# Second layer norm's refinements on VectorE, W's norm asked for sooner, and two instead of three ph products ahead of the first group of batch 0

## The chip, the cores and the metric

The kernel runs on one core of a Trainium2 chip. The metric is the device time of one execution in microseconds; the median of three runs of the kernel before is 919.04 us (917.95 to 919.18). Of the core's engines, TensorE does the matrix products, VectorE and ScalarE the elementwise work, GpSimd some very small elementwise work, and SyncE (SP) does no arithmetic: its queue issues every DMA of this kernel.

## The reference

A layer norm, a product with a context through a fake quantisation to 8 bits, a residual, a second layer norm, and a feed-forward product with bias, to which a routed low-rank part (the best two of eight experts) is added, with a second residual:

```python
q1 = fake_quant(layernorm(x), x1_scale, x1_zp)
q2 = fake_quant(ctx, x2_scale, x2_zp)
x = x + matmul(q1, q2)
xf = layernorm(x)
w = top2(softmax(xf @ W_router.T))
h = einsum('td,erd->ter', xf, lora_A)
lora_out = einsum('ter,eor,te->to', h, lora_B, w) * 2.0
x = x + xf @ W_base.T + b_base + lora_out
```

There are two batches of 1024 rows; all widths are 2048, in float32.

## The kernel before

The two batches run one after the other. A batch's 1024 rows are eight tiles of 128 rows, and two neighbouring tiles make a pair p (0 to 3). The columns are in two halves of 1024.

**First product.** In batch 0, `gemm1` (L772) takes tile after tile; `evac1` adds the result to x. In batch 1, `gemm1w` (L886) does it pairwise with fewer products. When the last columns of a tile are in, the sums for the second layer norm are there.

**Second layer norm.** `ln2` (L911) works on a pair p. Its `stat` (L920 to L927) makes mean and variance with a few VectorE instructions on a column or two, and a first guess of the reciprocal root (`seed`, L451). Its `newton` (L933) refines the guess in three steps (`rstd_steps`, L462) and then makes the scale `a` and the offset `mb` (L937 to L939). The line `fast = p >= 2` puts this on VectorE for pairs 2 and 3, one tile at a time, and on GpSimd for pairs 0 and 1, both tiles at once. A refinement step takes four instructions on GpSimd, three on VectorE for two tiles, and two on VectorE for one.

**y and its transposes.** `y_prep` (L943) makes seven matrices of each pair from its four quarters of y = (x - mean) * scale: a11 and a12 from the first tile, then a22, and the combinations s1 to s4 by VectorE (`comb`, L973). Each is split into a hi and a lo part in float16 (the lo part by VectorE, L965), named nat_... , and both are transposed by DMA into y_... (L407 for a half, L969 for a whole).

**Weights.** A piece of W is named by batch, half of W, group and k: w_0_0_2_6 belongs to batch 0, half 0, group 2, k = 6. `w_step` (L1136) loads its parts (wn, wt, wb, wc), combines them, and splits the scaled result: hi at L417 or L424, lo at L1158 on VectorE. The scale gW comes from the norm of W's half: `w_norm` (L601) loads sixteen pieces wn_15 to wn_0, sums their squares, adds them up over the partitions with a TensorE product wsum, and computes gW, uW and sB. It is called with a time: `w_norm(0, t - WN0)`, where t is the planned end of the first product.

**Feed-forward product.** `g2` (L1339) goes through two halves f, four groups in each, eight k in a group and four pairs; each is three matmuls of 128x512 into a PSUM bank X or Y. In the first half, group 0 takes a11 and a12 of y, group 1 s2 and s1, group 2 s3 and s4, group 3 a22. The bias is loaded as bb and added at L1267 in group 2.

**The ph products.** `hmm` (L1004) makes the router's and low-rank part's product ph_b_i of tile i (L1014, L1018; 32 matmuls, in two halves). For an even tile it takes a11 and a12, for an odd tile s1 and a22. `HFIRST[b]` names the tiles whose product stands ahead of the first group, `HLATE[b]` those which follow at the start of group 1 of the first half.

**What sets the order.** No engine's list is written by hand. Every piece of work is a task with an engine, an estimated duration and the buffers it reads and writes (`Plan.add`, L123). `rank` gives each a due time from those who need it, back from times given for TensorE's work, and `order` (L177) then lays out all five engines' lists by these due times while the kernel is built. Each engine executes its list strictly in order. So an estimate, a due time or the engine of one task can move others on every engine. SP's queue is such a list too: loads, stores and transposes wait for each other's turn, and each DMA uses one of eight lanes in rotation.

Of the kernel before, what the change touches and what calls it, by code (L numbers as in the profile page):

```python
# [18 lines left out]
ALU = mybir.AluOpType  # L19
# [6 lines left out]
D = 2048  # L26
# [16 lines left out]
         "sm": 4, "sm2": NP, "wacc": 1, "ps": 8}  # L43
HORIZON = 120.0
MM = 0.216
SPREAD = .75
LANES = 8
DEPTH = 2.5
NEAR = 45.0
WARM = 90  # L50
WFAR = 90.0
HFIRST = ((0, 1, 2), (0, 2, 4))
HLATE = ((4, 6, 3, 5, 7), (6, 1, 3, 5, 7))
EV1 = 5.0
QBOTH = 2
EV1W = 2.0
# [18 lines left out]
WKEEP0 = 8  # L75
PUT_W = 10
WN_STEP = 3.0
WN0 = 20.0
WN1 = 40.0
SPILL0 = 3  # L80
SP_T = 5.0
# [36 lines left out]
class Plan:  # L118
# [4 lines left out]
    def add(self, eng, dur, fn, r=(), w=(), prio=None, cap=None, dma=None, far=None, turn=False,  # L123
            store=False):
        t = Task()
        t.durs = eng if isinstance(eng, dict) else {eng: dur}
        t.eng, t.dur = None, min(t.durs.values())
        t.fn, t.prio, t.cap, t.dma = fn, prio, cap, dma
        t.preds, t.succs, t.bufs = set(), [], []
        t.seq, t.ready, t.start, t.done = len(self.tasks), 0.0, None, None  # L130
        if self.lead is not None:
            t.cap = self.lead
        t.pe = prio if eng == "PE" else None
        t.far, t.turn, t.store = far, turn, store
        t.whole = t.mate = None
        t.skip = False

        def spans(accs):
            for a in accs:
                buf, parts = a if isinstance(a, tuple) else (a, None)  # L140
                if buf not in t.bufs:
                    t.bufs.append(buf)
                    buf.users += 1
                for i in range(buf.parts) if parts is None else parts:
                    yield buf, i

        for buf, i in spans(r):
            last, readers = buf.state[i]
            if last is not None:
                t.preds.add(last)  # L150
            readers.append(t)
        for buf, i in spans(w):
            last, readers = buf.state[i]
            if last is not None:
                t.preds.add(last)
            t.preds.update(readers)
            buf.state[i] = (t, [])
        t.preds.discard(t)
        for p in t.preds:
            p.succs.append(t)  # L160
        self.tasks.append(t)
        return t
# [165 lines left out]
def xattn_ffn_kernel(ctx, tc, x, cx, scal, wT, bias, arT, bT, out):  # L328
    nc = tc.nc
# [5 lines left out]
    add = plan.add  # L335
# [325 lines left out]
    def ln1(S, b, i):  # L661
# [30 lines left out]
        if b:  # L692
# [8 lines left out]
            for h in range(2):  # L701
# [4 lines left out]
                        "p (k t s) -> p k s t", t=P, s=2),  # L706
                    HD, [(q, [2 + h])], [(aT, [h])], bias=nz1, dve=SPREAD)
        else:
# [18 lines left out]
        if first:  # L727
# [8 lines left out]

            add("PE", 2.0 + MM * WARM / 2, warm_up, w=[warm], prio=0.0)

# [33 lines left out]
    def gemm1(S, b, i, c, t):  # L772
# [3 lines left out]
        def mm(k0, n):  # L776
            for k in range(k0, k0 + n):
                nc.tensor.matmul(  # L778
                    ps.ap(), aT.ap()[:, k, :], S["b", c, k // 4].ap()[:, k % 4, :],
                    start=k == 0, stop=k == KT - 1,  # L780
                )

        n = 2 if b == 0 and c < 1 and i < 4 else 4
        for k0 in range(0, KT, n):
            bp = S["b", c, k0 // 4]
            parts = [k0 % 4 // 2] if n == 2 else [0, 1]
            at = t + k0 * MM
            if n == 2 and c == 0:
                at = t - i * KT * MM + LEAD * i + PACE * k0
            add("PE", n * MM, lambda k0=k0: mm(k0, n), r=[(aT, [k0 // HK]), (bp, parts)], w=[ps],  # L790
                prio=at)
        evac1(S, b, i, c, ps, t + KT * MM + EV1)
        if c % 2:
            squares(S, b, i, c)

    def evac1(S, b, i, c, ps, cap, total=True):
        xb = S["x", i][c // 2]
        p, j = i // 2, i % 2
        if ("s2", p) not in S:
            S["s2", p] = buf("sm2", [P, 52], F32, f"sm2_{b}_{p}", 2)  # L800
        s = S["s2", p]

        def evac():
            xs = xb.ap()[:, (c % 2) * C : (c % 2 + 1) * C]
            o = 14 + 4 * j + c
            kw = dict(accum_out=s.ap()[:, o : o + 1]) if total else {}
            nc.vector.scalar_tensor_tensor(xs, ps.ap(), s12, xs, ALU.mult, ALU.add, **kw)  # L807

        add("DVE", 0.75, evac, r=[ps], w=[(xb, [c % 2])] + ([(s, [j])] if total else []), cap=cap)
# [76 lines left out]
    def gemm1w(S, b, p, cp, grp, t):  # L886
        ops = GROUPS1[grp]
        for j, (bk, op, fresh) in enumerate(ops):
# [4 lines left out]
            for h in range(2):  # L893
# [9 lines left out]

                add("PE", 4 * MM, mm, r=[acc, w], w=[ps], prio=t + (8 * j + 4 * h) * MM)
            for bk2, tt, c, total in EVAC1[grp]:
# [4 lines left out]

    def ln2(S, b, p, js):  # L911
        s = S["s2", p]
        fast = p >= 2
        j0, n = js[0], len(js)

        def cut(o, w=1):
            v = s.ap()[:, o + j0 * w : o + (j0 + n) * w]
            return v if w == 1 else v.rearrange("p (j c) -> p j c", j=n)

        def stat():  # L920
            m, d, v, r, hv = cut(28), cut(30), cut(0), cut(4), cut(6)
            nc.vector.tensor_reduce(m, cut(14, 4), AX.X, ALU.add)
            nc.vector.tensor_reduce(v, cut(24, 2), AX.X, ALU.add)
            nc.vector.tensor_scalar(m, m, 1.0 / D, None, ALU.mult)
            nc.vector.tensor_tensor(d, m, cut(22), ALU.add)
            nc.vector.tensor_tensor(d, d, d, ALU.mult)
            nc.vector.scalar_tensor_tensor(v, v, 1.0 / D, d, ALU.mult, ALU.subtract)  # L927
            seed(v, r, hv)

        add("DVE", 1.5, stat, w=[(s, js)])  # L930

        def newton():
            e = nc.vector if fast else nc.gpsimd  # L933
            r, hv, t = cut(4), cut(6), cut(8)
            rstd_steps(e, r, hv, t, n)
            m, a, mb = cut(28), cut(10), cut(12)
            e.tensor_scalar(a, r, YS, None, ALU.mult)  # L937
            e.tensor_tensor(mb, m, a, ALU.mult)
            e.tensor_scalar(mb, mb, -1.0, None, ALU.mult)  # L939

        add("DVE" if fast else "POOL", 2.0 if fast else 4.8, newton, w=[(s, js)])

    def y_prep(S, b, p):  # L943
        s = S["s2", p]
# [470 lines left out]
    for b in range(NB):  # L1415
        S = {}
        for o in ("x0", "c0", "x1", "x2", "x3", "c1", "x4", "x5", "x6", "x7", "c2", "c3"):
            n = int(o[1])
            if o[0] == "x":
                plan.lead = lead(b, "x", n)  # L1420
                load_x(S, b, n)
                ln1(S, b, n)
                plan.lead = None
            else:
                load_b(S, b, n)
        if b == 0:
            for i, c in unit_order():
                gemm1(S, b, i, c, t)
                t += KT * MM
                if c == NC - 1:  # L1430
                    S["t_y", i] = t
        else:
            for p in range(NP):
                half_sums(S, b, p)
            for cp in range(2):
                half_diffs(S, b, cp)
            for p, cp, grp in BLOCKS1:
                gemm1w(S, b, p, cp, grp, t)
                t += 8 * MM * len(GROUPS1[grp])
                if cp and grp > 1:  # L1440
                    S["t_y", 2 * p + grp - 2] = t
        if b == 0:
            prep_lora(t - LORA_T)
            prep_bmax(t - LORA_T + 20.0)
            w_norm(0, t - WN0)
        for p in range(NP):
            for js in ([0], [1]) if p >= 2 else ([0, 1],):
                ln2(S, b, p, js)
            y_prep(S, b, p)
        for i in HFIRST[b]:  # L1450
            hmm(S, b, i, t)
            t += 2.8
        for f in range(2):
            cp = f if b == 0 else 1 - f
            for i in range(NT):
                reload(S, b, f, cp, i)
            for grp in range(4):
                if grp == 1:
                    if not f:
                        for i in HLATE[b]:  # L1460
                            hmm(S, b, i, t)
                            t += 2.8
                        router(S, b)
                if grp == 2 - f:
                    load_lb(S, b, cp, (1, 0, 2))
                if grp == 2:
                    add_bias(S, b, cp, t + BIAS)
                elif grp == 3:
                    if b == 0 and f == 0:
                        w_norm(1, t - WN1)  # L1470
                for k in range(HK):
                    w_step(S, b, f, cp, grp, k, t)
                    for p in range(NP):
                        lag = LAG3 if p == 3 else 0
                        g2(S, b, f, cp, grp, k, p, t + (0 if f or grp else lag * 24 * MM))
                        t += 3 * MM * len(GROUPS[f][grp])
                        if k == HK - 1:
                            t += 3 * MM * len(LORA[f][grp])
# [55 lines left out]
```

## Time and profile before

| | |
|---|---|
| median of three runs | 919.04 us |
| profiled execution | 917.52 us |
| its span | 915.7 us |
| mean granted TensorE clock | 0.994 |
| GpSimd | busy 67.1 us (7%), 256 instructions |
| ScalarE | busy 399.9 us (44%) |
| TensorE | busy 897.4 us (98%) |
| first matmul of the first group of batch 0 | 150.43 us |

All times in the text that are not durations count from the start of the span. The profile names engines PE (TensorE), PEld (its weight loads), DVE (VectorE), ACT (ScalarE), POOL (GpSimd) and SPq (SP's DMA queue). A row of the timeline has the start, the duration, the engine, the source line, the operation, what it writes and reads, and, in brackets, how long the engine had been idle before it and what ended that. A group row has the busy time and mean duration in ns of one, then the idle time just before such instructions and its commonest cause. Names of buffers stand there without their numbers.

### The profile page before, as it was taken

The page shows a single profiled execution, that of the slowest core. Times are in us where ns is not written, and L with a number is a line of the kernel's source. Part 1 is how long each engine was busy: PE and PEld are TensorE (multiplying, and loading weights), DVE is VectorE, ACT ScalarE, POOL GpSimd, SP SyncE. Part 2 cuts the span into 40 slices and gives each one's busy share as a digit, 9 for nine tenths or more (in the row PEclk, how much of TensorE's full clock was granted, in tenths as well). Part 3 has the DMA queues.
Part 4 walks back from the last instruction along what each step waited for, and adds up shares of the span by engine and source line. Part 5 has one row for each costly group of instructions (what it writes and reads, how often), then busy time and mean ns, then how long its engine had stood idle before and what let it go on. Part 6 is the DMA issues. An engine that isn't in the chain of part 4 may idle for free.

```text
span 915.7 us, 12485 instructions
## 1 busy us (share of the span) xinstructions
PE 897.4 (98%) x4514; PEld 431.3 (47%) x4514; DVE 712.6 (78%) x1271; ACT 399.9 (44%) x454; POOL 67.1 (7%) x256
## 2 busy tenths in 40 slices
PE   7999998999999999999999999899999999999998
PEld 5444445474444444444444444547444444444443
DVE  7999989999599975899899987899734453899131
ACT  5998677516044321414696667853100121234000
POOL 0024220000000000002470001000000000000000
PEclk9999999999999999999999999999999999999999
DMA  8999999997999999999999647999996169793021
GB/s 322 387 386 295 304 275 237 220 227 253 231 332 332 409 375 368 363 376 365 346 350 299 204 164 200 242 201 179 309 234 210 58 208 393 257 347 124 4 91 47
DMA packets 223981, 241.02 MB, mean 263 GB/s; under 512 B 146096, under 2 KB 158384, under 8 KB 223920
## 3 DMA queue, kind: packets, MB, share of 16 engines
q1 hardware_dynamic: 223920, 240.23, 86.6%
q8 instruction: 35, 0.57, 0.3%
q14 instruction: 26, 0.21, 0.1%
HBM read 163.65 MB, written 41.94 MB: 225 GB/s over the span
## 4 chain that ended last, share of the span: by engine, by line
PE 86%; DVE 7%; DMA 4%; issue 1%; POOL 1%; SPq 0%; ACT 0%; DVEq 0%
PE X L1348 36%; PE Y L1348 27%; PE g L778 6%; PE gX L898 5%; PE gY L898 4%; PE ph L1014 2%; PE X L1364 2%; PE Y L1364 2%; DMA bs<-in_cx_dram 1%; PE ph L1018 1%; DMA wn<-in_wT_dram 1%; DVE x L807 1%; DMA y_a<-nat_a 1%; DVE nat_a L965 1%; DMA wc<-in_wT_dram 1%
## 5 line engine op out<-in xcount | busy, mean ns | idle before, releaser
L1348 PEld LDWEIGHTS <-y_s 128*128 128x128 f16 x1536 | 150.2, 98 | 180.8
L1348 PE MATMUL Y<-w,y_s 128*128 128x512 f16 x768 | 206.8, 379 | 0.0
L1348 PE MATMUL X<-w,y_s 128*128 128x512 f16 x768 | 206.5, 379 | 0.0
L1348 PE MATMUL X<-w,y_a 128*128 128x512 f16 x768 | 189.9, 380 | 1.2 <-DVE w L1158 0.7
L1348 PEld LDWEIGHTS <-y_a 128*128 128x128 f16 x1152 | 112.5, 98 | 134.3 <-issue 3.1
L778 PE MATMUL g<-b,at 128*128 128x512 f16 x512 | 114.3, 383 | 4.5 <-ACT b L417 2.5
L417 ACT ACTIVATE w<-wb,gW 128x1024 f16<-128x1024 f32 (+1 forms) x47 | 50.7, 1084 | 128.9 <-DVE wb L1219 56.9
L1348 PE MATMUL Y<-w,y_a 128*128 128x512 f16 x384 | 103.6, 380 | 0.0
L1376 DVE SCALAR_TENSOR_TENSOR xr<-X,uW,xr 128x512 f32<-128x512 f32 x64 | 46.7, 744 | 50.2 <-PE X L1348 25.5
L778 PEld LDWEIGHTS <-at 128*128 128x128 f16 x512 | 49.9, 99 | 64.7 <-issue 4.5
L1158 DVE SCALAR_TENSOR_TENSOR w<-wb,gW,w 128x1024 f16<-128x1024 f32 (+1 forms) x48 | 56.9, 1190 | 7.3 <-ACT w L417 7.2
L1376 DVE SCALAR_TENSOR_TENSOR xr<-Y,uW,xr 128x512 f32<-128x512 f32 x42 | 31.0, 743 | 35.1 <-PE Y L1364 35.0
L417 ACT ACTIVATE b<-u,nz 128x1024 f16<-128x1024 uint8 x40 | 45.0, 1139 | 15.5 <-DVE bt L869 13.8
L467 POOL TENSOR_TENSOR sm<-sm 128x1 f32<-128x1 f32 (+1 forms) x48 | 12.8, 266 | 480.7 <-DVE sm L453 476.9
L417 ACT ACTIVATE w<-wt,gW 128x1024 f16<-128x1024 f32 x14 | 16.1, 1148 | 63.6 <-DVE wt L1205 37.2
L417 ACT ACTIVATE yt_a<-x,sm 128x1024 f32<-128x1024 f32 x28 | 33.4, 1231 | 23.4 <-POOL sm L939 13.7
L440 DVE BATCH_NORM_STATS2 sm<-x 128x6 f32<-128x512 f32 x64 | 40.8, 680 | 3.0 <-DMA x<-in_x_dram 2.9
L417 ACT ACTIVATE nat_s<-yt_a 128x1024 f16<-128x1024 f32 x29 | 30.0, 1050 | 24.8 <-DVE yt_a L973 20.6
L417 ACT ACTIVATE q<-x,sm 128x1024 uint8<-128x1024 f32 x30 | 35.7, 1230 | 11.3 <-POOL sm L677 8.0
L826 ACT ACTIVATE sq<-x,sm 128x1024 uint8<-128x1024 f32 x32 | 36.3, 1136 | 9.0 <-DVE x L807 9.0
L417 ACT ACTIVATE u<-bs,sc,rec 128x1024 uint8<-128x1024 f32 x31 | 38.0, 1231 | 3.6 <-DMA bs<-in_cx_dram 3.4
L1018 PE MATMUL ph<-ar,y_a 128*128 128x136 f16 x192 | 35.3, 225 | 4.2 <-DMA y_a<-nat_a 4.1
(191 smaller groups left out, 1160.9 us busy)
## 6 DMA issues: line engine op xcount, KB each, us to landing
bs<-in_cx_dram SPq DMA_DIRECT2D x64, 512.0 KB, 9.4
wt<-in_wT_dram SPq DMA_DIRECT2D x64, 512.0 KB, 7.2
wn<-in_wT_dram SPq DMA_DIRECT2D x32, 512.0 KB, 9.5
x<-in_x_dram SPq DMA_DIRECT2D x30, 512.0 KB, 8.3
spill<-x SPq DMA_DIRECT2D x28, 512.0 KB, 3.6
xr<-spill SPq DMA_DIRECT2D x28, 512.0 KB, 8.1
wb<-in_wT_dram SPq DMA_DIRECT2D x24, 512.0 KB, 8.0
out_dram<-xr SPq DMA_DIRECT2D x24, 512.0 KB, 5.7
```

What stands on the lines that cost most here:

```text
L417: nc.scalar.activation(o, i, AF.Copy if c is None else AF.Identity, scale=1.0 if a is None else a, bias=0.0 if c is None else c,)
L440: nc.vector.bn_stats(st[:, 2 * h + c], b.ap()[:, c * C : (c + 1) * C])
L467: e.tensor_tensor(t, r, r, ALU.mult)
L778: nc.tensor.matmul(ps.ap(), aT.ap()[:, k, :], S["b", c, k // 4].ap()[:, k % 4, :], start=k == 0, stop=k == KT - 1,)
L826: nc.scalar.activation(sq.ap(), xb.ap(), AF.Square, bias=a[:, 22 + j : 23 + j], accum_out=a[:, 24 + 2 * j + h : 25 + 2 * j + h],)
L898: nc.tensor.matmul(ps.ap(), a()[:, 4 * h + k, :], w.ap()[:, k, :], start=fresh and h + k == 0, stop=h == 1 and k == 3, skip_group_check=True,)
L1014: nc.tensor.matmul(ph.ap()[:, : 2 * AR], y[half].ap()[:, 0, k, :], ar[:, kr, :], start=kk == 0, stop=False,)
L1018: nc.tensor.matmul(ph.ap()[:, AR : 2 * AR], y[half].ap()[:, 1, k, :], ar[:, kr, :AR], start=False, stop=kk == KT - 1,)
L1158: lambda: nc.vector.scalar_tensor_tensor(w.ap()[:, 1, lo:up], src(), g, w.ap()[:, 0, lo:up], ALU.mult, ALU.subtract),
L1348: nc.tensor.matmul(ps.ap(), y.ap()[:, a, k, :], w.ap()[:, q, j * C : (j + 1) * C], start=k == 0 and fresh and i == 0, stop=k == HK - 1 and ...
L1364: nc.tensor.matmul(ps.ap(), hT.ap()[:, 2 * p + tt, a], lb.ap()[:, q], start=fresh and i == 0, stop=i == 2, skip_group_check=True,)
L1376: nc.vector.scalar_tensor_tensor(xs, ps.ap(), uW[:, cp : cp + 1], xs, ALU.mult, ALU.add)
```

## The change

It touches constants at the top, `ln2`, and the loop that calls it.

- The refinement of pairs 0 and 1 goes to VectorE in both batches, still for both tiles at once (`NEWTON`, `SPLIT`).
- The division of the mean by D is folded into the instruction after it, in `stat`, and into the offset in `newton`, where two instructions become one on VectorE. The planner's estimates for the two tasks are lowered by 0.2 each.
- `WN0` is 30 instead of 20: the work of W's first norm is due ten us sooner.
- In batch 0, tile 1's ph product moves from `HFIRST` to `HLATE`, behind tiles 4 and 6.

```diff
--- before.py
+++ after.py
@@ -43,14 +43,16 @@
          "sm": 4, "sm2": NP, "wacc": 1, "ps": 8}
 HORIZON = 120.0
 MM = 0.216
+NEWTON = (0, 0)
+SPLIT = (2, 2)
 SPREAD = .75
 LANES = 8
 DEPTH = 2.5
 NEAR = 45.0
 WARM = 90
 WFAR = 90.0
-HFIRST = ((0, 1, 2), (0, 2, 4))
-HLATE = ((4, 6, 3, 5, 7), (6, 1, 3, 5, 7))
+HFIRST = ((0, 2), (0, 2, 4))
+HLATE = ((4, 6, 1, 3, 5, 7), (6, 1, 3, 5, 7))
 EV1 = 5.0
 QBOTH = 2
 EV1W = 2.0
@@ -75,7 +77,7 @@
 WKEEP0 = 8
 PUT_W = 10
 WN_STEP = 3.0
-WN0 = 20.0
+WN0 = 30
 WN1 = 40.0
 SPILL0 = 3
 SP_T = 5.0
@@ -910,7 +912,7 @@
 
     def ln2(S, b, p, js):
         s = S["s2", p]
-        fast = p >= 2
+        fast = p >= NEWTON[b]
         j0, n = js[0], len(js)
 
         def cut(o, w=1):
@@ -921,13 +923,12 @@
             m, d, v, r, hv = cut(28), cut(30), cut(0), cut(4), cut(6)
             nc.vector.tensor_reduce(m, cut(14, 4), AX.X, ALU.add)
             nc.vector.tensor_reduce(v, cut(24, 2), AX.X, ALU.add)
-            nc.vector.tensor_scalar(m, m, 1.0 / D, None, ALU.mult)
-            nc.vector.tensor_tensor(d, m, cut(22), ALU.add)
+            nc.vector.scalar_tensor_tensor(d, m, 1.0 / D, cut(22), ALU.mult, ALU.add)
             nc.vector.tensor_tensor(d, d, d, ALU.mult)
             nc.vector.scalar_tensor_tensor(v, v, 1.0 / D, d, ALU.mult, ALU.subtract)
             seed(v, r, hv)
 
-        add("DVE", 1.5, stat, w=[(s, js)])
+        add("DVE", 1.3, stat, w=[(s, js)])
 
         def newton():
             e = nc.vector if fast else nc.gpsimd
@@ -935,10 +936,13 @@
             rstd_steps(e, r, hv, t, n)
             m, a, mb = cut(28), cut(10), cut(12)
             e.tensor_scalar(a, r, YS, None, ALU.mult)
-            e.tensor_tensor(mb, m, a, ALU.mult)
-            e.tensor_scalar(mb, mb, -1.0, None, ALU.mult)
-
-        add("DVE" if fast else "POOL", 2.0 if fast else 4.8, newton, w=[(s, js)])
+            if fast:
+                e.scalar_tensor_tensor(mb, m, -1.0 / D, a, ALU.mult, ALU.mult)
+            else:
+                e.tensor_tensor(mb, m, a, ALU.mult)
+                e.tensor_scalar(mb, mb, -1.0 / D, None, ALU.mult)
+
+        add("DVE" if fast else "POOL", 1.8 if fast else 4.8, newton, w=[(s, js)])
 
     def y_prep(S, b, p):
         s = S["s2", p]
@@ -1444,7 +1448,7 @@
             prep_bmax(t - LORA_T + 20.0)
             w_norm(0, t - WN0)
         for p in range(NP):
-            for js in ([0], [1]) if p >= 2 else ([0, 1],):
+            for js in ([0], [1]) if p >= SPLIT[b] else ([0, 1],):
                 ln2(S, b, p, js)
             y_prep(S, b, p)
         for i in HFIRST[b]:
```

## The prediction

> **What bounds the kernel now.** I read the page's busy shares first, then every hole in TensorE's timeline, then, for each hole, the engine or queue that closed it.
>
> ```profile
> PE 897.4 (98%) x4514; PEld 431.3 (47%) x4514; DVE 712.6 (78%) x1271; ACT 399.9 (44%) x454; POOL 67.1 (7%) x256
> ...
> L417 ACT ACTIVATE yt_a<-x,sm 128x1024 f32<-128x1024 f32 x28 | 33.4, 1231 | 23.4 <-POOL sm L939 13.7
> ...
> L1018 PE MATMUL ph<-ar,y_a 128*128 128x136 f16 x192 | 35.3, 225 | 4.2 <-DMA y_a<-nat_a 4.1
> ```
>
> TensorE is idle for 915.7 - 897.4 = 18.3 us. The change can reach neither the first load (6.6) nor the tail after the last matmul (3.8). The rest is three places. The second row says that ScalarE's first y tiles wait for GpSimd's refinement, the third that the ph products wait for transposes of y_a. The timeline of TensorE shows where:
>
> ```profile
> 143.94 0.29 PE L1014 MATMUL ph<-ar,y_a 128*128 128x272 f16 x1 [0.25 <-DMA y_a<-nat_a]
> ...
> 147.53 0.29 PE L1014 MATMUL ph<-ar,y_a 128*128 128x272 f16 x1 [2.02 <-DMA y_a<-nat_a]
> 148.55 0.23 PE L1018 MATMUL ph<-ar,y_a 128*128 128x136 f16 x1 [0.73 <-DMA y_a<-nat_a]
> ...
> 581.18 0.23 PE L1018 MATMUL ph<-ar,y_a 128*128 128x136 f16 x1 [3.36 <-DMA y_a<-nat_a]
> ```
>
> So 3.0 us stand in batch 0 inside ph_0_2, ahead of the first FFN group (150.43), and 3.36 us in batch 1 inside ph_1_2. Two more waits for split weights, 0.51 and 0.67, come at 311. The busy time by stretch, from the view of windows (busy and count of PE, weight loads, DVE, ACT, POOL, then the clock):
>
> ```profile
> 149.20:152.70 3.50, 3.50 (x16) 1.85 (x14) 3.16 (x5) 2.46 (x4) 0.00 (x0) 0.51 1.04 198
> ...
> 260.00:285.00 25.00, 25.00 (x118) 11.33 (x116) 24.55 (x62) 15.12 (x25) 0.00 (x0) 1.00 1.02 334
> ...
> 581.20:584.60 3.40, 3.40 (x35) 2.78 (x36) 0.10 (x1) 1.18 (x2) 0.00 (x0) 1.00 1.13 220
> ```
>
> The first hole is followed by 3.5 us at a clock of 0.51, worth 1.7 us; the hole of batch 1 is not (1.00). And from 260 to 285 VectorE is busy 24.55 of 25 us: TensorE does not wait there, but only just. I took each weight piece's first matmul against the end of its VectorE part: group 1 of batch 0 has 9.5 to 20 us in hand, w_0_0_2_2 (first used at 258.76) 1.22, w_0_0_2_3 0.53, w_0_0_2_6 only 0.04. What starts that stretch is SP's queue and then VectorE:
>
> ```profile
> 222.16 2.00 SPq L969 DMA_TRANSPOSE y_s<-nat_s  x1
> 224.25 0.86 SPq L398 DMA_DIRECT2D xr<-spill  x1
> 225.21 3.58 SPq L407 DMA_TRANSPOSE y_s<-nat_s  x2
> ...
> 246.25 0.54 SPq L398 DMA_DIRECT2D bb<-in_bias_dram  x1
> 246.84 0.45 SPq L398 DMA_DIRECT2D wc<-in_wT_dram  x1
> ```
>
> ```profile
> 251.11 2.36 DVE L1267 TENSOR_TENSOR xr<-xr,bb 128x1024 f32<-128x1024 f32 x2 [1.68 <-DMA bb<-in_bias_dram]
> ```
>
> From 222.16 transposes stand back to back until the bias (bb) and wc_0_0_2_2 are issued, and VectorE idles 1.68 us for the bias. Later here is later for the batch.
>
> **The change part by part.**
>
> *Refinements to VectorE.* The four refinements that move took GpSimd, in its timeline, 6.3 us (93.86 to 100.13) and 7.1 (115.06 to 122.19) in batch 0, 4.2 each (546.43, 560.00) in batch 1. VectorE's refinement of pair 3 runs nine small instructions from 142.16 to 144.03, 0.21 each; for two tiles it is 3 x 3 + 2 = 11, 2.3 us. Four add 9.2; the folded scale removes 12 + 8 instructions, 4.0. So VectorE gains 5.2 us of work, and each pair's scale comes 4.0 to 4.8 us sooner in batch 0 and 1.9 in batch 1, if VectorE is free. Here a rule speaks against the change: the Trainium skill (Perfetto Trace Analysis, Optimizing Scalar/DVE Operations) says that with a saturated VectorE some work may be better off on ScalarE or even GpSimd. Over the stretches where batch 0's refinements land (95 to 136) VectorE is busy 36.9 of 41 us, so by the rule up to 5.2 us could be lost; by the rows TensorE waits for nothing there, the added work fits the 4.1 idle, and its cost is 0. I go by the rows; the rule returns below, at 260 to 285.
>
> *W's norm sooner.* The ten last wn loads of W's half are issued from 110.84 to 119.41, and the two transposes behind them take 12.53 us on SP where the next two take 3.09. Built, the changed order has them ahead of every y transpose; the last would land near 122 instead of 132. The scale gW then hangs on the last layer-norm piece instead: TensorE's first product ends near 139.5, behind it on VectorE come an eviction (0.74), a residual (1.2), statistics (1.2), the scale (1.3), an eviction (0.74), two hi parts (0.75 each) and w_0_0_0_0's lo part (1.28). That gives 146 against 149.45. Bounds 145 and 148.3; I take 146, 3.5 sooner.
>
> *ph_0_1 later.* Its 32 matmuls (140.11 to 142.9, 2.8 us) move to group 1's start; nothing is saved. TensorE would be through ph_0_2 at 150.43 - 3.0 - 0.6 (half clock) - 2.8 = 144, and wait for w_0_0_0_0 until 146. The stall of y_a12_0_1 goes, since its transpose is now ahead by some 12 us; the weight is late next, by 2. Group 0 starts 4.5 sooner, group 1, behind ph_0_1, 1.7 sooner. The clock may keep its full rate too; this cannot show in the end, as the next step says.
>
> *What is pushed behind.* In the changed lists pair 0's y_s1 and y_a22 are made after the first group starts. SP gets their four transposes (1.3 to 2 us each) between 157 and 200, ahead of group 1's weights, whose 9.5 to 20 us cover them. VectorE, between w_0_0_0_0 and w_0_0_1_7 (223.29), gets four combinations and two lo parts of pair 0 (6 x 1.14), pair 3's first refinement (1.9), three pieces of its y (2.1), two ph sums (0.5), one hi part (0.75), less one copy and two moved operations (3.0): 9. It starts 3.5 sooner and has idle time of 2.04 (182.06), 0.27, 0.63 and 0.80 to take it up; since TensorE's end of group 0 comes sooner too, I count 2.7 of 3.7. So w_0_0_1_7 comes at +2.8. Behind it stand, in the changed order, nat_s4_0_0 and a combination of pair 3 (2.3), for which the xr load ahead of y_s4_0_0 waits. y_s4_0_0 is issued at 223.3 + 2.8 + 2.3 + 0.9 = 229.3 instead of 225.21: **+4.1**. Bounds: +0.8 if VectorE takes up everything (then the queue waits for TensorE's end with w_0_0_1_3, 227.68 - 1.7), +6 if it takes up nothing more than 1. From there to w_0_0_2_7 both kernels have the same SP and VectorE lists. w_0_0_2_2 is then ready at 261.7, TensorE arrives at 258.76 - 1.7 = 257.1 and stalls 4.6; at w_0_0_2_6 it is 4.1 late, with no slack left to hide it.
>
> *The clock behind that stall.* The Trainium skill (TensorE: Matmul & The Clock Gate, Why this matters for your kernels) warns of idle gaps over about 3 us, which send the clock to half. Here 3.36 us did not (1.00 after 581.2) and 3.0 in three pieces did. By the rule the 4.6 costs 1.7 more, by the row of batch 1 nothing; since the next weights are late on VectorE anyway, at most about 0.5 of it shows. I take 0.4.
>
> *Batch 1.* y_a12_1_1's last transpose is issued at 577.65, behind lo parts that VectorE did at 570.86 and 571.99 and a spill that waited until 574.49. In the changed order those lo parts stand right behind three evictions and pair 1's refinement, some 4 us sooner, the spill stands behind the transposes, and TensorE has its leftover products between the two halves of ph_1_2. The 3.36 should go: -3.0, bounds -1 (VectorE, 3.53 of 3.7 busy at the hole, too late) and -3.4. The weights of batch 1 have 4 us and more in hand.
>
> Sum: 4.1 + 0.4 - 3.0 = +1.5. The profiled execution took 917.52 (span 915.7, 1.8 around it), 1.5 under the median of 919.04, so it would become 919.0, and the median **920.5**.
>
> **Rivals.**
> - *The queue keeps its time* (other side). VectorE's idle places take up all nine us and y_s4_0_0 slips 0.8 only, so TensorE's slip at w_0_0_2_6 is 0.8 and batch 1 gives 3.4: 919.04 - 2.6 = 916.4. It decides when y_s4_0_0 slips less than 2.6. For it: group 1's weights leave VectorE room; against: it is busy 66.6 of 71.5 us from 150.5 to 222.
> - *Batch 1 keeps its hole, or gets another*, as VectorE is 95% busy ahead of it: +4.5, 923.5. Against: its lists there put the needed lo parts first.
> - *The change only moves the holes*: 2 us of waiting for w_0_0_0_0 and 1 at w_0_0_2_2 for 3.0 and 3.36 with half a gain in batch 1: 919. The slack of 0.04 speaks against a small slip there.
>
> **How the numbers follow.** Forecast 0.50, queue keeps its time 0.28, batch 1 keeps its hole 0.14, moved holes 0.08. What a measurement can tell from no change is about 0.2%, 1.8 us. The forecast's own range is 918.8 to 922.6, with half of it or more beyond the 1.8. With the rivals: 915.8 to 923.6; faster 0.28, same 0.28, slower 0.44.
>
> **What would show it.** Right: no wait for y_a in ph_0_2, a wait of about 2 for w at the first group, a wait of 3 to 5 for w near 257 (L1348, by VectorE L1158), the bias issued near 250, no hole in ph_1_2, GpSimd without 128x2 refinements of the second layer norm. Wrong: bias issued at or before 248, or the hole of batch 1 still there, or a new one for y of pair 3 near 163, where the cover is some 3 us before and less after.

## The result, and the profile after

| | before | after |
|---|---|---|
| median of 6 runs, same chip | 919.11 us (917.95 to 920.15) | 922.69 us (921.18 to 923.51) |
| ratio, 95% interval | 1 | 1.0038 [1.0021, 1.0054] |
| profiled execution, span | 917.52, 915.7 | 921.18, 919.3 |
| granted clock, mean | 0.994 | 0.990 |

The changed kernel is slower by 3.5 us (0.0038 x 919; by the interval 1.9 to 5.0). The page of after, in the rows that answer to those of before (the first is busy us, share and instructions by engine; the other is a group: out<-in, shape, count, then busy us, mean ns, idle us before it and what ended it):

```profile
PE 900.2 (98%) x4514; PEld 432.2 (47%) x4514; DVE 718.0 (78%) x1297; ACT 398.1 (43%) x452; POOL 49.9 (5%) x196
...
L1018 PE MATMUL ph<-ar,y_a 128*128 128x272 f16 x192 | 37.0, 285 | 2.7 <-DMA y_a<-nat_a 2.7
```

VectorE has 5.4 us more (5.2 counted), GpSimd 17.2 less. TensorE's matmuls are the same 4514; they are busy 2.8 us longer, which goes with the lower clock, and its idle time is 919.3 - 900.2 = 19.1 against 18.3. So the holes have moved, not gone. TensorE's timeline of after (start, us, instruction, in brackets the idle time before it and its releaser) has these, and none at the first group:

```profile
255.44 0.38 PE L1352 MATMUL X<-w,y_s 128*128 128x512 f16 x1 [1.83 <-ACT w L419]
257.73 1.01 PE L1352 MATMUL X<-w,y_s 128*128 128x512 f16 x2 [1.92 <-DVE w L1162]
...
586.76 0.29 PE L1018 MATMUL ph<-ar,y_a 128*128 128x272 f16 x1 [2.65 <-DMA y_a<-nat_a]
587.63 0.30 PE L1022 MATMUL ph<-ar,y_a 128*128 128x136 f16 x1 [0.59 <-DMA y_a<-nat_a]
```

The first two are one stall of 3.75 us at w_0_0_2_2, the last two a hole of 3.24 inside ph_1_4, where before had one of 3.36 inside ph_1_2. (In these rows ACT w L419 is ScalarE's hi part of the weight, DVE w L1162 VectorE's lo part.) Read at TensorE's first product of each stage, the difference grows in two places only. (The third column is a second profiled execution of the same changed kernel, taken later.)

| TensorE starts (us) | before | after | after, again |
|---|---|---|---|
| w_0_0_0_0 (first FFN group) | 150.43 | 143.40 | 143.55 |
| w_0_0_1_0 (group 1) | 206.31 | 201.64 | 201.79 |
| w_0_0_2_2 (behind the stall) | 258.76 | 255.44 | 258.01 |
| w_0_0_3_0 | 295.02 | 296.44 | 297.73 |
| w_0_1_0_0 (end of batch 0's first half) | 322.56 | 323.98 | 325.27 |
| w_1_1_1_0 (batch 1) | 641.78 | 645.20 | 647.80 |
| end of the last matmul | 911.95 | 915.37 | 917.97 |

In batch 0 a lead of 7.0 us at the first group, 4.7 at group 1, becomes a loss of 1.4 (again: 2.7). From w_0_1_0_0 to w_1_1_1_0 it takes 319.22 before, 321.22 after (again: 322.53), a loss of 2.0 (3.3). From there to the last matmul all three take 270.17. The third column also shows how far two profiles of one kernel can lie apart: 2.6 us. So below a place is read from profiles, a cost from the ratios.

How the lead is lost shows on SP's queue in after (the same three issues that were shown of before, up to the bias):

```profile
222.22 1.94 SPq L973 DMA_TRANSPOSE y_s<-nat_s  x1
224.49 0.71 SPq L400 DMA_DIRECT2D xr<-spill  x1
225.30 3.73 SPq L409 DMA_TRANSPOSE y_s<-nat_s  x2
...
246.29 0.57 SPq L400 DMA_DIRECT2D bb<-in_bias_dram  x1
```

and in VectorE's timeline, which waits for it:

```profile
251.24 2.36 DVE L1271 TENSOR_TENSOR xr<-xr,bb 128x1024 f32<-128x1024 f32 x2 [6.75 <-DMA bb<-in_bias_dram]
```

The bias is issued at 246.29 where it was 246.25 before: the queue has kept its time to 0.04 us although TensorE is 4.7 ahead, so VectorE idles 6.75 us for it instead of 1.68, and TensorE arrives early at a weight that is not earlier. In the second profile of after it is issued at 248.73.

What sets the queue is the stretch between the first group and those transposes, as far as the traces tell. The view of windows of before, and then of after (length; busy us and count of PE, weight loads, DVE, ACT, POOL; clock; DMA share; GB/s):

```profile
146.00:222.00 76.00, 73.74 (x438) 40.18 (x439) 71.13 (x103) 40.97 (x46) 0.00 (x0) 0.98 1.03 241
```

```profile
146.00:222.00 76.00, 76.00 (x468) 41.93 (x467) 73.79 (x104) 38.66 (x42) 0.00 (x0) 1.00 0.90 217
```

VectorE is busy 73.79 of 76 us (97%), though over the whole span its share is 78%. TensorE does not wait in this stretch either (76.00 of 76). But what SP's queue waits for comes from VectorE, and with VectorE full, TensorE's lead does not make it come sooner. No run changes VectorE's load in this stretch alone, so this reading rests on d1 and a3 below, which move work into and out of it.

The loss from w_0_1_0_0 to w_1_1_1_0 is another matter. The windows of before, and then of after, over just this stretch:

```profile
322.56:641.78 319.22, 315.73 (x1615) 152.70 (x1613) 278.76 (x477) 167.52 (x178) 38.65 (x150) 1.00 0.95 287
```

```profile
323.98:645.20 321.22, 317.44 (x1615) 153.56 (x1614) 283.06 (x492) 166.85 (x177) 32.54 (x120) 0.99 0.95 288
```

Of the 2.0 us only 0.3 is waiting (321.22 - 317.44 = 3.78 against 3.49). The other 1.7 is TensorE being busy longer with the same 1615 products: behind its hole after has 3.41 us at half clock (0.50 from 587.08 to 590.49), and before has none there. More on this under the clock below.

### The profile page after: what moved, and what is told of

It reads as the page before. It is cut to its first block, busy times and chain, and to the rows that moved or that the text cites. A ratio compares the mean times of both kernels' runs of the same rounds, so it can differ in the third digit from the quotient of the medians.

```text
span 919.3 us, 12454 instructions
## 1 busy us (share of the span) xinstructions
PE 900.2 (98%) x4514; PEld 432.2 (47%) x4514; DVE 718.0 (78%) x1297; ACT 398.1 (43%) x452; POOL 49.9 (5%) x196
## 4 chain that ended last, share of the span: by engine, by line
PE 73%; DVE 12%; DMA 6%; ACT 3%; issue 2%; POOL 1%; SPq 1%; DVEq 0%; ACTq 0%; POOLq 0%
PE X L1352 32%; PE Y L1352 24%; PE g L780 7%; PE ph L1018 2%; PE X L1368 2%; PE Y L1368 2%; DVE x L809 2%; PE gX L900 2%; DVE w L1162 1%; DMA wc<-in_wT_dram 1%; PE ph L1022 1%; DMA wt<-in_wT_dram 1%; PE gY L900 1%; DMA bs<-in_cx_dram 1%; DVE sm L442 1%
## 5 line engine op out<-in xcount | busy, mean ns | idle before, releaser
L419 ACT ACTIVATE w<-wb,gW 128x1024 f16<-128x1024 f32 (+1 forms) x46 | 49.6, 1082 | 121.5 <-DVE wb L1223 57.8
L780 PEld LDWEIGHTS <-at 128*128 128x128 f16 x512 | 49.8, 98 | 64.7 <-issue 3.7
L1162 DVE SCALAR_TENSOR_TENSOR w<-wb,gW,w 128x1024 f16<-128x1024 f32 (+1 forms) x48 | 56.8, 1190 | 7.3 <-ACT w L419 7.2
L419 ACT ACTIVATE b<-u,nz 128x1024 f16<-128x1024 uint8 x40 | 45.0, 1139 | 15.3 <-DVE bt L871 13.8
L419 ACT ACTIVATE nat_s<-yt_a 128x1024 f16<-128x1024 f32 x32 | 33.0, 1051 | 30.3 <-DVE yt_a L977 24.0
L419 ACT ACTIVATE w<-wt,gW 128x1024 f16<-128x1024 f32 x14 | 16.1, 1148 | 64.9 <-DVE wt L1209 40.6
L419 ACT ACTIVATE q<-x,sm 128x1024 uint8<-128x1024 f32 x30 | 35.7, 1231 | 11.3 <-POOL sm L679 7.3
L419 ACT ACTIVATE u<-bs,sc,rec 128x1024 uint8<-128x1024 f32 x31 | 38.0, 1232 | 4.7 <-DMA bs<-in_cx_dram 4.1
L1018 PE MATMUL ph<-ar,y_a 128*128 128x272 f16 x192 | 37.0, 285 | 2.7 <-DMA y_a<-nat_a 2.7
L900 PEld LDWEIGHTS <-at 128*128 128x128 f16 x256 | 24.9, 98 | 30.5 <-issue 1.5
L1271 DVE TENSOR_TENSOR xr<-xr,bb 128x1024 f32<-128x1024 f32 x28 | 33.4, 1216 | 6.8 <-DMA bb<-in_bias_dram 6.8
L977 DVE TENSOR_TENSOR yt_a<-yt_a,yt_a 128x1024 f32<-128x1024 f32 x32 | 38.5, 1215 | 0.0
```

The source lines that it names most:

```text
L419: nc.scalar.activation(o, i, AF.Copy if c is None else AF.Identity, scale=1.0 if a is None else a, bias=0.0 if c is None else c,)
L780: nc.tensor.matmul(ps.ap(), aT.ap()[:, k, :], S["b", c, k // 4].ap()[:, k % 4, :], start=k == 0, stop=k == KT - 1,)
L900: nc.tensor.matmul(ps.ap(), a()[:, 4 * h + k, :], w.ap()[:, k, :], start=fresh and h + k == 0, stop=h == 1 and k == 3, skip_group_check=True,)
L977: add("DVE", 1.22, lambda: nc.vector.tensor_tensor(dst.ap(), a.ap(), c.ap(), op), r=[a, c], w=[dst])
L1018: nc.tensor.matmul(ph.ap()[:, : 2 * AR], y[half].ap()[:, 0, k, :], ar[:, kr, :], start=kk == 0, stop=False,)
L1162: lambda: nc.vector.scalar_tensor_tensor(w.ap()[:, 1, lo:up], src(), g, w.ap()[:, 0, lo:up], ALU.mult, ALU.subtract),
```

## The experiments

Each theory's expectation was written before its run. Times are differences from before, from the ratio of the runs of one chip; 1 us is 0.11%.

How far can a place in one profile be trusted? Up to w_0_1_0_0, after, its repetition (e3), b1 and, but for its added products, a4 have the same instruction lists on every engine. Their bias is issued at 246.29, 248.73, 246.20 and 247.64, and they reach w_0_1_0_0 at 323.86 to 325.27. d1 and e1 also share one list there: bias at 243.12 and 245.78, w_0_1_0_0 at 320.43 and 322.51. So the two lists differ clearly, but a shift of 2.5 us or less between two single profiles (a1, a2, a3, e4 against their partners) is a hint only.

**Which part costs?** Each part alone, and the changed kernel with one part undone.

*a1: the refinements alone* (the changed kernel less the other two parts).

```diff
-HFIRST = ((0, 2), (0, 2, 4))
-HLATE = ((4, 6, 1, 3, 5, 7), (6, 1, 3, 5, 7))
-WN0 = 30
+HFIRST = ((0, 1, 2), (0, 2, 4))
+HLATE = ((4, 6, 3, 5, 7), (6, 1, 3, 5, 7))
+WN0 = 20.0
```

> Only the refinements on VectorE and the folded scale, with W's norm and the ph products as before. Theory C (the changed kernel's 3.6 us are two clock drops behind stalls, 1.3 in batch 0 at w_0_0_2_2 and about 2 in batch 1): W's ten wn loads still hold up the first transposes, so TensorE does not reach group 0 much sooner, no stall at w_0_0_2_2, batch 0 within 0.7 of before; batch 1 has the changed kernel's lists or nearly, a hole near 584 and 2 us more. Sum +1 to +2.5: 920.1 to 921.6. Theory V (5.2 us more work on VectorE makes both batches late): +3 to +4 already here, 922 to 923.

Measured: 918.87, ratio 1.0000 [0.9985, 1.0016]: no change, a miss of both theories. In its profile batch 0 is 0.8 shorter (bias at 244.19), batch 1 is 1.2 longer, with a hole of 2.34 + 0.61 in ph_1_4 and 3.4 us at half clock behind it. The refinements and the folded scale alone bring the hole's new place.

*a2: W's norm alone*, on the kernel before.

```diff
-WN0 = 20.0
+WN0 = 30
```

> Only W's norm asked for 10 us sooner. Theory C: what TensorE gains ahead of group 0 is hidden at w_0_0_2_2, since bias and wc_0_0_2_2 still come near 246.5; up to 3 us sooner there costs no long stall. Batch 1 as before. Within 1 of before: 918.1 to 920.1. Theory V: no work added to VectorE, 919.1 as well; so this tells only whether this part alone can cost anything.

Measured: 917.82, 0.9977 [0.9963, 0.9992]: faster by 2.1, where both theories gave at most 1. Bias at 244.60, 1.65 sooner; the hole in ph_1_2 stays (3.39).

*a3: ph_0_1 late alone*, on the kernel before.

```diff
-HFIRST = ((0, 1, 2), (0, 2, 4))
-HLATE = ((4, 6, 3, 5, 7), (6, 1, 3, 5, 7))
+HFIRST = ((0, 2), (0, 2, 4))
+HLATE = ((4, 6, 1, 3, 5, 7), (6, 1, 3, 5, 7))
```

> Only ph_0_1 moved behind the first group in batch 0. Theory C: ahead of group 0 TensorE waits longer for y_a12_0_1 and the weight (2.8 us less work to fill), group 1 comes at about the same time as before, nothing changes at w_0_0_2_2; within 1 of before, 918.1 to 920.1. Rival P (the missing filler is what costs): +2 to +3, 921 to 922.

Measured: 921.13, 1.0020 [1.0006, 1.0035]: slower by 1.8, outside the plus or minus 1 that my theory gave, nearer to its rival. The first group starts at 143.58 here, as early as in the whole change, and the bias comes late. SP's timeline of a3:

```profile
247.76 0.62 SPq L398 DMA_DIRECT2D bb<-in_bias_dram  x1
```

That is 1.5 later than before. TensorE then stalls at w_0_0_2_2 (0.62 + 1.87) and once more at 288 (1.71); batch 0 ends 3.7 later.

*d1: the whole change less the late ph_0_1* (HFIRST and HLATE as before, the rest changed).

```diff
-HFIRST = ((0, 2), (0, 2, 4))
-HLATE = ((4, 6, 1, 3, 5, 7), (6, 1, 3, 5, 7))
+HFIRST = ((0, 1, 2), (0, 2, 4))
+HLATE = ((4, 6, 3, 5, 7), (6, 1, 3, 5, 7))
```

> The changed kernel with ph_0_1 back ahead of the first group. Theory B (batch 0 ends by the issue of the bias on SP, which came 2.1 sooner with the refinements alone, 1.65 sooner with W's norm alone and 1.5 later with ph_0_1 moved alone): bias issued between 242.5 and 244.5 instead of 246.29, batch 0 3 to 4 sooner than in the changed kernel, batch 1 as there (+2 against before). Time 918.3 to 919.8. Theory S (the three parts add up in time: 0 and -2 here): 917 to 917.5. If the ph move is harmless: 922.7.

Measured: 918.22, 0.9999 [0.9987, 1.0011]: ph_0_1's move was not harmless. Batch 0 ends 3.55 sooner than in after, as said. Batch 1 was expected at +2, but takes 319.04 here, 0.2 less than before, though the hole in ph_1_4 is there (2.49 + 0.61). SP's timeline and the windows of d1:

```profile
218.67 2.00 SPq L973 DMA_TRANSPOSE y_s<-nat_s  x1
...
243.12 0.55 SPq L400 DMA_DIRECT2D bb<-in_bias_dram  x1
```

```profile
146.00:222.00 76.00, 75.04 (x447) 40.33 (x446) 75.00 (x110) 41.30 (x45) 0.00 (x0) 1.00 0.94 234
```

VectorE is as full (75.00 of 76), but the transpose of 222.22 is at 218.67, the bias 3.2 sooner than in after. When the first group starts, VectorE has finished two combinations and eight lo parts of y in d1, none and seven in after. With ph_0_1 late, what it needs lies behind that start, inside the full stretch; with ph_0_1 early it lies ahead.

*b1: the whole change, but batch 1's refinements back on GpSimd.*

```diff
-NEWTON = (0, 0)
+NEWTON = (0, 2)
```

> The changed kernel with batch 1's refinements of pairs 0 and 1 back on GpSimd. Batch 1's lists of transposes and loads are then as before or nearly. Theory B: the bias near 246.3 and batch 0 at +1.4 (W's second half begins 1.4 later than before), batch 1 back to the time of before, its hole in ph_1_2 again: +1.0 to +1.8, 920.3 to 921.3. If batch 1's refinements on VectorE were a gain, as predicted: 925.

Measured: 918.56, 1.0007 [0.9994, 1.0020]. Batch 0 as in after (+1.3); from w_0_1_0_0 to w_1_1_1_0 317.78, and of the hole only 1.27 + 0.27 is left. The return of the hole in ph_1_2, and with it 920.3 to 921.3, was expected and did not come.

*b2: batch 1's refinements alone on VectorE*, with the folded scale (HFIRST, HLATE and WN0 as before).

```diff
-NEWTON = (0, 0)
+NEWTON = (2, 0)
```

> Before with batch 1's refinements of pairs 0 and 1 on VectorE alone (and the folded scale in both batches). Theory B: batch 0 as before; a hole of about 3 in ph_1_4 in place of that in ph_1_2, and +1 to +3: 920 to 922. If the prediction's gain of batch 1 exists at all: 916 to 918.

Measured: 920.50, 1.0020 [1.0007, 1.0033]: slower by 1.8. Batch 0 ends as before (322.63); batch 1 is 2.2 longer. TensorE's timeline of b2 has the hole of after, and none in ph_1_2:

```profile
585.32 0.29 PE L1018 MATMUL ph<-ar,y_a 128*128 128x272 f16 x1 [3.28 <-DMA y_a<-nat_a]
586.22 0.29 PE L1022 MATMUL ph<-ar,y_a 128*128 128x136 f16 x1 [0.61 <-DMA y_a<-nat_a]
```

*e1: both costs taken out*: ph_0_1 early, batch 1's refinements on GpSimd.

```diff
-HFIRST = ((0, 2), (0, 2, 4))
-HLATE = ((4, 6, 1, 3, 5, 7), (6, 1, 3, 5, 7))
-NEWTON = (0, 0)
+HFIRST = ((0, 1, 2), (0, 2, 4))
+HLATE = ((4, 6, 3, 5, 7), (6, 1, 3, 5, 7))
+NEWTON = (0, 2)
```

> The changed kernel without its two costly parts: ph_0_1 back ahead of the first group, batch 1's refinements of pairs 0 and 1 back on GpSimd. Theory B (ph costs about 3.5 by VectorE's late work of pair 0, batch 1's refinements about 3, the rest gains): batch 0 ends 2 to 3 sooner than before, batch 1 as before or 1 to 2 sooner, 915 to 916.5, the first that beats both. If the two costs overlap (each taken away alone already brought back nearly all): 918 to 919.

Measured: **915.52** (914.55 to 917.04), 0.9959 [0.9944, 0.9974]: 3.8 faster than before, and the fastest kernel of this study. But not where it was expected: the bias is at 245.78, in this profile batch 0 ends as before (322.51; d1, with the same list, 2.1 sooner), and batch 1 is 3.0 shorter. Part of the lead goes with the clock: all nine executions have a mean of 0.996, the 32 of before on this chip 0.9938 on average, which is 2.0 us of lost clock less. With this run the four corners are complete:

| difference from before (us) | batch 1's refinements on GpSimd | on VectorE |
|---|---|---|
| ph_0_1 ahead of the first group | -3.8 (e1) | -0.1 (d1) |
| ph_0_1 behind it | +0.6 (b1) | +3.5 (after) |

Moving ph_0_1 costs 4.4 in the first column and 3.6 in the second; moving batch 1's refinements costs 3.7 in the first row and 2.9 in the second. Within the noise the two costs add. Each interval is about 1.3 wide to either side, so the sizes are good to some 2 us, the signs are clear.

*e4: e1 with ph_0_1 third instead of second.*

```diff
-HFIRST = ((0, 1, 2), (0, 2, 4))
+HFIRST = ((0, 2, 1), (0, 2, 4))
```

> As e1_no_ph_no_b1, but with ph_0_1 third of the three ahead of the first group, behind ph_0_2. Theory B: pair 0's s1 and a22 are still made ahead of the first group, so the bias is no later than with the old order (242.5 to 244.5), and TensorE has a product more to fill until w_0_0_0_0; within 1.5 of e1_no_ph_no_b1. If what counts is that pair 0's other matrices come behind pair 1's: the bias 1 to 2 later and the time 1 to 2 above e1_no_ph_no_b1.

Measured: 917.98, 0.9986 [0.9972, 0.9999]: 2.5 worse than e1, where theory B gave at most 1.5. Bias at 247.98 (one profile). The other reading fits better: even ahead of the first group, a later place of ph_0_1 costs.

*e3: the changed kernel again, unchanged*, for the spread of a profile.

> The changed kernel once more, beside the others on this chip. 922.5 (921.5 to 923.5). In its trace the bias is issued between 246.3 and 247.7, as the kernels built from it showed; a stall at w_0_0_2_2 and a hole of 2.5 to 3.3 in ph_1_4 again; whether the clock is at half behind each may differ from the first profile.

Measured: 922.77, 1.0042 [1.0026, 1.0059]; the stalls are 2.06 + 1.92 at w_0_0_2_2 and 2.90 + 0.59 in ph_1_4, at the same places. The bias came later than expected, at 248.73.

**Is it the clock?** In after, the clock is low behind both stalls: 0.50 from 256 to 262.5, 0.66 from 586 to 591. *a4* keeps TensorE busy in them. It adds products with a matrix of zeros, which add nothing to the sums: 16 ahead of w_0_0_2_2, 14 ahead of pair 2's products in ph_1_4 (shown without the lookup of the two places).

```diff
+    zero = const.tile([P, P], F16)
+    nc.gpsimd.memset(zero, 0.0)
...
+            if k in at:
+                b, n = at[k]
+                for _ in range(n):
+                    nc.tensor.matmul(b.ap(), zero, wide[:, :C], start=False, stop=False,
```

> The changed kernel with 16 matmuls of zeros, 512 columns each, ahead of w_0_0_2_2's first product (3.5 us into a stall of 3.75) and 14 ahead of ph_1_4 (3.0 us into a hole of 3.2); they add nothing to the sums. Theory C: TensorE is no more idle there, the clock stays at 1.00 behind both places, and the time falls by 0.8 in batch 0 (then the weights of VectorE are the limit, 0.6 late) and by 1.2 to 1.7 in batch 1: 919.9 to 920.7. Theory V (late VectorE or transposes are the whole cost): no change or somewhat slower, 922.7 to 923.

Measured: 922.79, 1.0041 [1.0025, 1.0058], against 1.0038 for after. The two windows of after, then of a4:

```profile
256.00:262.50 6.50, 4.77 (x12) 1.69 (x12) 6.21 (x8) 1.61 (x4) 0.00 (x0) 0.50 1.02 338
...
586.00:591.00 5.00, 3.66 (x20) 2.44 (x21) 4.57 (x16) 5.00 (x6) 0.00 (x0) 0.66 1.07 230
```

```profile
256.00:262.50 6.50, 5.84 (x28) 2.57 (x27) 6.50 (x8) 3.96 (x6) 0.00 (x0) 1.00 1.04 383
...
586.00:591.00 5.00, 4.18 (x29) 2.31 (x28) 3.90 (x18) 5.00 (x7) 0.00 (x0) 1.00 0.97 175
```

The clock is full at both places and the time is the same; the 919.9 to 920.7 of theory C lies outside the interval. In batch 0 the reason can be seen. VectorE (third pair) is busy 6.50 of 6.50 in the first window: what TensorE gains in speed it waits for again, at the weights that VectorE finishes one after another. The last of those that TensorE waits for, in a4's timeline of TensorE:

```profile
281.09 0.59 PE L1354 MATMUL X<-w,y_s 128*128 128x512 f16 x2 [0.30 <-DVE w L1164]
```

That is w_0_0_2_6, ready at 281.04 (after: 280.02). b1 shows the same without added products. Its lists are those of after up to w_0_1_0_0, but its clock stayed full. The windows from w_0_0_2_2 to w_0_0_3_0, of after and then of b1:

```profile
255.44:296.44 41.00, 39.08 (x169) 16.89 (x169) 38.46 (x79) 20.27 (x33) 0.00 (x0) 0.92 1.02 317
```

```profile
254.96:296.32 41.36, 36.91 (x169) 16.31 (x168) 38.50 (x79) 20.35 (x33) 0.00 (x0) 1.00 1.01 322
```

TensorE is busy 2.2 us less and waits 2.5 us more; it reaches w_0_1_0_0 at 323.86, after at 323.98. In these two profiles the half clock of batch 0 costs nothing.

In batch 1 it is otherwise, and a4 cannot tell: its 14 products take 3.19 us, 0.17 + 0.65 of waiting is left around them, and other waits (1.2, at 503 to 529) fall into the same stretch. Better is to compare profiles. From w_0_1_0_0 to w_1_1_1_0, d1, a1, b2 and b3 have the lists of after on every engine; a3 has those of before, and a2 too but for two loads.

| w_0_1_0_0 to w_1_1_1_0 (us) | length | TensorE idle | at half clock |
|---|---|---|---|
| list of after: d1 | 319.04 | 3.19 | none |
| b3 | 319.28 | 3.32 | none |
| a1 | 320.43 | 3.04 | 3.4 |
| after | 321.22 | 3.78 | 3.4 |
| b2 | 321.39 | 3.98 | 3.4 |
| after, again | 322.53 | 4.54 | 3.4 |
| list of before: a3 | 318.46 | 3.00 | none |
| before | 319.22 | 3.49 | none |
| a2 | 321.64 | 3.39 | 6.8 |

At full clock the new list is as long as the old one. With 3.4 us at half clock it is longer by about the 1.7 us that these lose and by what it idles more: behind the hole, TensorE waits for nothing up to w_1_1_1_0, so nothing hides it. (a2, with 6.8, is 2.4 longer than before.) d1's window shows the full clock, to be read against that of after above:

```profile
320.43:639.47 319.04, 315.85 (x1614) 152.68 (x1613) 283.37 (x492) 166.69 (x177) 32.53 (x120) 1.00 0.95 290
```

So theory C falls for batch 0, and for batch 1 the clock is most of what the profiles show. Whether the new list draws the half clock more often than the old stays open: the mean clock of b2's executions is 0.9918 against 0.9938 for before on its chip, worth 1.8 us, as much as b2 costs; but d1 and a1, with the same list, are no lower than before.

**Can the wait be mended where it shows?** *b3* moves the bias and wc_0_0_2_2 ahead of the transpose of y_s3_0_2 on SP.

```diff
+    for name in ("bb_0_0", "wc_0_0_2_2"):
+        t = tasks.pop(find("SP", name))
+        tasks.insert(find("SP", "y_s3_0_2"), t)
```

> The changed kernel with two loads moved on SP, the bias and wc_0_0_2_2 ahead of y_s3_0_2's transpose instead of behind y_s4_0_3's. Theory B: the bias is issued near 236, VectorE does its additions in the 6.75 us in which it waited for it, w_0_0_2_2 is ready before TensorE comes (253.6), no stall of 3.75 and no half clock behind it; batch 0 ends 4 to 6 sooner: 916.7 to 919. Theory V (VectorE is 98% busy from 260 to 285 whatever comes first): at most 1 sooner, 921.7 to 922.7.

Measured: 923.02 (919.00 to 925.93, six runs), 1.0053 [1.0032, 1.0074]: no gain. The profile is that of the fastest run, at 919.00. The bias is 9.6 sooner, and the wait reappears on VectorE one operation further. SP's and VectorE's timelines of b3:

```profile
236.68 0.53 SPq L400 DMA_DIRECT2D bb<-in_bias_dram  x1
```

```profile
255.57 1.23 DVE L617 SCALAR_TENSOR_TENSOR wn<-wn 128x1024 f32<-128x1024 f32 x1 [6.22 <-DMA wn<-in_wT_dram]
```

A norm piece (wn_1_15) stands ahead of the weight's lo part in VectorE's list, its load is still behind the transposes (issued at 250.86), and the idle 6.75 has become 6.22. w_0_0_2_6 is ready at 280.83, 0.8 later.

*c1* also moves, in batch 1, the loads wc_1_1_0_3 to 5 behind the transposes of y_a12_1_2 on SP, and ScalarE's hi parts of w_1_1_0_3 and 4 with them.

```diff
+    at = [tasks[find("SP", f"wc_1_1_0_{k}")] for k in (3, 4, 5)]
+    at += [tasks[find("ACT", f"w_1_1_0_{k}")] for k in (3, 4)]
+    for t in at:
+        tasks.remove(t)
+    n = find("SP", "y_a12_1_2", True) + 1
+    tasks[n:n] = at
```

> As b3_bias, and in batch 1 the loads wc_1_1_0_3 to 5 stand behind y_a12_1_2's transpose instead of ahead of y_a11_1_2's (and ScalarE's hi parts of w_1_1_0_3 and 4 behind that). Theory L (batch 1's new hole of 3.2 in ph_1_4 is those three loads ahead of the transposes): hole under 1, no half clock behind it, 2.5 to 4 below b3_bias: 913 to 916. If the hole comes from VectorE's lo part of y_a11_1_2 (done at 578.9): at most 1.5 below b3_bias.

Measured: 925.71, 1.0079 [1.0059, 1.0099], worse. The hole in ph_1_4 is gone, so those loads had a part in it, but TensorE's timeline of c1 has new ones:

```profile
591.88 0.81 PE L1352 MATMUL Y<-w,y_a 128*128 128x512 f16 x3 [2.90 <-DVE x L809]
607.59 0.82 PE L1352 MATMUL X<-w,y_a 128*128 128x512 f16 x3 [1.56 <-DMA y_a<-nat_a]
```

The first waits for one of VectorE's evictions (results taken out of PSUM into x). The holes are longer than the one removed.

## Why the prediction was half right

The forecast was 920.5 and "slower" the likeliest sign. 922.69 is slower, 0.1 above the forecast's own range (to 922.6) and inside the wider one (to 923.6). That it came so near is luck: two errors had opposite signs. Batch 0 was put at +4.5 with the clock and measured +1.4 and +2.7 in two profiles; batch 1 was put at -3.0 and measured +2.0 and +3.3. One of the prediction's own signs of being wrong appeared, the bias at or before 248 (246.29; 248.73 in the second profile).

- **Refinements at no cost in batch 0: held, as far as shown.** The work added was 5.4 us (5.2 said). With the refinements alone (a1) batch 0 ends 0.8 sooner in the profile. No run has batch 0's refinements without anything else.
- **W's norm sooner: right way, too small.** w_0_0_0_0 was ready at 143.36, outside my bounds of 145 to 148.3; so the wait of 2 at the first group did not come, and the group started 7.0 sooner, not 4.5. The pieces that I listed add up to 147.5; 146 leaves out the two hi parts. And the chain was the wrong one: the first product ended at 139.4, as said, but statistics stood ahead of its end and no residual behind it. The scale was made by 140.17, and only one eviction, two hi parts and the lo part followed.
- **The push behind group 0: right mechanism, mis-sized and put at the wrong door.** y_s4_0_0 was issued at +0.09 (second profile +2.55) instead of +4.1, which fits a first group, and with it VectorE's stretch, that began 7.0 us sooner instead of 4.5. But the right comparison is not with before. The sooner norm and the refinements had won time that ph_0_1's move then gave away: against d1 the bias is 3.2 later (246.2 to 248.7 in four executions of the one list, 243.1 and 245.8 in two of the other). I charged the loss to the sum and overlooked the gain of the parts without it.
- **A stall at w_0_0_2_2 of 4.6: 3.75 measured**, 1.92 of it for VectorE as named, 1.83 for ScalarE's part of the same weight. TensorE's early arrival bought nothing, as said.
- **The clock behind the stall, +0.4.** The rule of the Trainium skill (TensorE: Matmul & The Clock Gate, Why this matters for your kernels) that gaps over about 3 us halve the clock described the stall of batch 0 (3.75 in two pieces, 0.50 after it) and of ph_1_4 (3.24 in two pieces, 0.66). It did not describe the 3.36 in ph_1_2 before (1.00 after it), nor e4, where gaps of 0.24 and 1.87 were followed by 0.53 from 259.4 to 263. In batch 0 the price was nil, as who is late next decides there. For batch 1 I took the row of before and put the clock at nothing; it cost 1.7 of the 2.0 us.
- **Batch 1's hole goes, -3.0: the step that failed.** Its own argument came true: y_a12_1_1 is transposed by 575.03, and ph_1_2 has no hole. But a hole of the same size (3.24 for 3.36) opened in ph_1_4, and half clock behind it, which the sum did not have, made +2.0 of it. I stopped at the first hole, and asked of the next transpose only whether the weights had slack. SP's timeline of after shows what is late next:

```profile
575.13 1.08 SPq L400 DMA_DIRECT2D wc<-in_wT_dram  x2
576.29 0.42 SPq L400 DMA_DIRECT2D spill<-x  x1
576.80 1.46 SPq L400 DMA_DIRECT2D wc<-in_wT_dram  x1
578.37 7.25 SPq L409 DMA_TRANSPOSE y_a<-nat_a  x2
```

and VectorE's, in the same stretch:

```profile
574.63 2.47 DVE L1162 SCALAR_TENSOR_TENSOR w<-wc,gW,w 128x1024 f16<-128x1024 f32 x2
...
577.69 2.35 DVE L969 TENSOR_TENSOR nat_a<-yt_a,nat_a 128x1024 f16<-128x1024 f32 x2
```

Three weight loads and a spill stand ahead of pair 2's transposes, and two lo parts of weights (2.47, L1162) ahead of the lo parts of y that they wait for (L969). In e1, with the refinements on GpSimd, these lo parts of y stand first and those of the weights behind. VectorE's own work hardly differs; the windows of after, then of e1:

```profile
560.00:586.00 26.00, 24.10 (x150) 13.23 (x148) 23.55 (x65) 16.44 (x20) 0.00 (x0) 1.00 1.05 250
```

```profile
560.00:586.00 26.00, 26.00 (x168) 14.48 (x166) 22.72 (x60) 20.65 (x25) 2.70 (x14) 1.00 1.02 245
```

0.83 us more on VectorE, and TensorE has 1.90 us of holes in the window instead of none, and the rest of after's hole behind it. The planner gives VectorE its order by the costs it is told. The lists show that the refinements' move changed the order, and c1 that the hole goes when three loads stand elsewhere; that the order and not the added work made the hole is argued, not shown. "Batch 1 keeps its hole, or gets another", given 14%, named this and came nearest: 923.5 said, 922.69 measured. Its number was lucky too, since it kept +4.5 for batch 0. Its reason for (VectorE 95% busy ahead of the hole) was in the profile. The Trainium skill (Perfetto Trace Analysis, Optimizing Scalar/DVE Operations) says that with a full VectorE some work may be better off elsewhere: I weighed it for batch 0, where it did not bite, and left it out for batch 1, where b1 and b2 put the move at 2 to 3 us, clock included.

Two things stay open. Before and e1 differ in batch 1 only by the folded scale and by the lists that follow from it and from batch 0, and yet its hole falls from 3.36 to 0.54 us (b1 and e4, with the same VectorE list: 1.54 and 2.18 in two pieces); whether the fold's work or the reshuffled list does it was not tried apart. And the four parts alone (about -2.1 for W's norm, -1.8 for batch 0's refinements as a1 less b2, +1.8 for ph_0_1, +1.8 for batch 1's refinements) add up to about zero, not to +3.5. The corners say that each of the two costs is larger once the gains are there (3.6 to 4.4 and 2.9 to 3.7 instead of 1.8), which fits a full VectorE with less slack, but no run shows it directly; with intervals of 1.3 to 1.6 us to either side, part of the gap may be noise.

## What to carry to other kernels

Getting TensorE to a stage sooner is worth nothing if another engine's full stretch sets what comes after: measure that engine's busy share in the stretch (97% here, 78% over the span), and follow the issue time of the load that ends the stretch, not TensorE's start. When a step of yours removes a hole, price the next transfer in the same queue before you book the gain, and half clock behind the next hole if TensorE waits for nothing after it. And take a bundle of edits apart: here two parts gained, two lost, and the kernel with the gaining ones alone is 3.8 us faster than before.

## What the runs showed that was not expected

- The same loss of clock costs nothing or all of it, by what comes next. In batch 0, after had 0.50 for about 6.5 us and b1, with the same lists, 1.00, and they reached w_0_1_0_0 0.12 us apart. In batch 1, 3.4 us at half clock made the stretch 1.7 us longer, since TensorE waited for nothing behind it.
- Executions of one list differ in the clock: behind the hole in ph_1_4, four profiles have half clock and two (d1, b3) do not.
- Two transposes took 7.25 us of SP's queue behind three weight loads and a spill, though VectorE's parts (L969) were done at 578.91 and 580.04; at 225.30 in the same execution two in a row took 3.73. The cause stays open.
